# Norms with one activation table, a second attention pass over two PSUM pools, moved value matmuls, one mask product on VectorE, and another order of PSUM banks

## The chip, the cores and the metric

The kernel runs on one core of a Trainium2 chip. The metric is the device time of one execution in microseconds (us). The program computes in 32-bit floats. Its engines are named as in the profile: PE (TensorE, the matmuls), PEld (its weight loads), DVE (VectorE), ACT (ScalarE), POOL (GpSimd) and SP (SyncE, which issues most transfers). Each engine works through its own queue in order and waits on semaphores of the others. A 32-bit matmul shows in the profile as two passes, so "x16" in a row of PE is eight matmuls in the program.

## The reference, cut to what matters

Two layers over 128 latent rows of width 256, with a context of 12544 rows of width 256. Each sublayer works on a layer norm of its input and is added to it:

```python
x = x + _L0_xattn_ref(_layernorm(x), ctx, mask, Wq, Wkv, Wo)      # 4 heads of 64, masked softmax over 12544
x = x + _L0_attn_ref(_layernorm(x), ...)                          # gated delta net, 12 heads
x = x + _L0_ffn_ref(_layernorm(x), ...)                           # 8 experts, top 1
x = x + _L1_xattn_ref(_layernorm(x), ctx, Wq, bq, Wk, bk, Wv, bv) # 16 heads of 16
x = x + _L1_attn_ref(_layernorm(x), ...)                          # linear attention with decay, gate
x = x + _L1_ffn_ref(_layernorm(x), ...)                           # 8 experts, top 2

def _layernorm(x, axis=-1, eps=1e-05):
    m = jnp.mean(x, axis=axis, keepdims=True)
    v = jnp.var(x, axis=axis, keepdims=True)
    return (x - m) / jnp.sqrt(v + eps)
```

## The kernel before

The context is cut into 25 blocks of 512 rows (the last has 256), `BLOCKS`; all of them stay in SBUF. The order of the work on PE and ACT, in the first attention on DVE too, is the order in which the program writes it down (`manual_schedule`); POOL and the rest are ordered by a scheduler.

**First attention** (`xattn0_first`). PE first runs twelve spare matmuls (L371), then the keys of block 0 (`keys`, L404, into PSUM tile `pk`, copied to `kT` by ACT). The layer norm of x runs meanwhile, and calls a function handed to it (`fill`) with a number at certain places; here that function only computes the keys of block 0 when the number is 4. Then come the transposes of h (L151), the queries (`pq`, L485; scaled into `qT` by ACT, L489), scores of block 0 (`sc`, L499), of which DVE takes row maxima (L502), the values of block 0 (`values`, L417, tile `pv`), diagonals of the maxima (L510), keys of block 1, and `pn`, which spreads the maxima (L513, copied to `nm`). From there the loop takes blocks in pairs: values and keys, the weighted sum of the last pair (`weigh`, L465, tile `ot`), scores of this pair (`scores`, L438, tile `st`). A pair has four tiles of weights e: DVE subtracts the maximum (L444), ACT takes the exp (L445), POOL turns the mask's bytes into floats (`mk`, L447, two buffers) and multiplies (L451), DVE adds to the sums (L456). PSUM has three double banks for `pk`, `pv`, `st` and the like (`x0_mm`), and a pool `x0_ot` for `spare` and `ot`, opened after it.

**Fillers.** The keys and values of the second attention (`keys1`, `values1`: L1027 and L1048, copied out by ACT in L1034 and L1053) depend only on the context. `Filler.steps` yields them in small units (two passes or so of keys, two matmuls of values), and `fill(n)` puts n units on PE wherever the middle layers leave it idle. They go through two PSUM banks of their own (`k1_ps`, in place of the first attention's pools when these are closed). The middle layers are the delta net (`delta_net`, six banks) and the experts (`experts`). `layernorm` calls `fill` with 1, 4 and 1, and by `rsqrt` (L126 to L132) with 2 and 2, ten units in all; there ACT takes the logarithm and then the exponential, each after loading a table (`preload_act_table_set`) of its own.

**Second attention** (`xattn1_first`). Norm, queries, an estimate of the maxima on 128 rows (`sa`, `against`), then `fill(None)`: all units that are left, on PE one after another. Then the pools are closed and `weigh1` runs over 98 chunks of 128 context rows: `scores(i)` (L1101) writes four strips of scores, one into the tile `st1` (one buffer) and three into `st3` (two buffers), ACT takes the exps (L1107, one of 512 and one of 1536 columns), `attend(i)` (L1118) adds the weighted values into `ot`, which a zeroing matmul (L1091) has opened. The order on PE is scores 0, 1, 2, attend 0, scores 3, attend 1 and so on. One pool, `x1_st`, holds all of these tiles.

**Last layers** (`last_layers`). Here PE waits for chains of small operations; `beat(n)` puts 2n passes of a matmul on it whose result nobody reads (L1359). `root` is the norm: logarithm and exponential from one table, loaded at the end of the pass over the context (L1137), and on DVE one step of Newton's method on the inverse root (L1351, L1365).

If a check of the sums finds them out of bounds, the whole network is run once more by another path; with these inputs it is not.

Of the kernel before, what the change touches and what calls it, by code (L numbers as in the profile page):

```python
# [23 lines left out]
S = 128  # L24
# [48 lines left out]
def network(ctx: ExitStack, tc: tile.TileContext, a: dict, y_out, bad):  # L73
# [47 lines left out]

    def rsqrt(dst, src, bias, scale=1.0, fill=None):


        if fill:
            nc.scalar.preload_act_table_set("natural_log")  # L126
            fill(2)
        nc.scalar.activation(dst, src, AF.Ln, bias=bias, scale=scale)
        if fill:
            nc.scalar.preload_act_table_set("exp_and_others")  # L130
            fill(2)
        nc.scalar.activation(dst, dst, AF.Exp, scale=-0.5)  # L132

    def layernorm(x, psum, tag, fill=None):
# [5 lines left out]
        rstd = small.tile([S, 1], F32, tag="ln_rstd", name="ln_rstd")  # L140
        if fill:
            fill(1)
        rsqrt(rstd, mv[:, 1:2], eps[:S, 0:1], fill=fill)
# [205 lines left out]
    def xattn0_first(ahead, ok, filler, rest):  # L349
# [5 lines left out]
        with (  # L355
# [3 lines left out]
            tc.tile_pool(name="x0_s", bufs=1) as sp,  # L359
            tc.tile_pool(name="x0_mm", bufs=3, space=PSUM) as ps_mm,  # L360
            tc.tile_pool(name="x0_ot", bufs=1, space=PSUM) as ps_ot,
# [48 lines left out]
            def values(b):  # L410
                vs[b] = kvp.tile([128, 4, D], F32, tag="v", name="v")
                pv = two("pv")
                for i in range(BLOCKS[b][1] // 256):
                    for c in range(2):
# [12 lines left out]
            def scores(b):  # L427
# [4 lines left out]
                for c0 in range(0, n // 128, 2):  # L432
# [18 lines left out]
                    nc.gpsimd.tensor_mul(e, e, mk.unsqueeze(1).to_broadcast([128, 4, 2, S]))  # L451
# [28 lines left out]
            hT = layernorm(x, ps_one, "mm", lambda n: keys(0) if n == 4 else None)  # L480
            qT = wp.tile([128, 2, S], F32, name="qT")
            pq = two("pq")
            for m in range(2):
                for k in range(KC):
                    nc.tensor.matmul(  # L485
                        pq[:, m, :S], wq[:, k, m * 128 : (m + 1) * 128], hT[:, k, :],
                        start=(k == 0), stop=(k == KC - 1),
                    )
            nc.scalar.mul(qT, pq[:, :, :S], DH**-0.5)  # L489
# [16 lines left out]
            values(0)  # L506
# [67 lines left out]
    def delta_net(x, wqkv, fill):  # L574
# [7 lines left out]
        with (  # L582
# [136 lines left out]
            nc.scalar.preload_act_table_set("exp_and_others")  # L719
# [216 lines left out]
    def experts(x, wr, bias_row, we, be_src, top, y=None, fill=lambda n: None):  # L936

        with (
# [9 lines left out]
            hT = layernorm(x, psp, "ps", fill)  # L948
# [115 lines left out]
    def weigh1(x, qs, kss, cp, sp, loaded, late):  # L1064
# [4 lines left out]
        with (  # L1069
            tc.tile_pool(name="x1_e", bufs=1) as ep,  # L1070
            tc.tile_pool(name="x1_st", bufs=1, space=PSUM) as ps_st,
# [17 lines left out]

            ot = ps_st.tile([128, G, S], F32, name="ot")  # L1090
            nc.tensor.matmul(ot.rearrange("p g s -> p (g s)"), zl, zr, start=True, stop=False)  # L1091
# [50 lines left out]
            pt = ps_st.tile([128, 1, G, S], F32, tag="st1", name="pt")[:, 0].rearrange("p g s -> p (g s)")  # L1142
# [55 lines left out]
    def xattn1_first(x, wq, filler, close, late):  # L1198
# [3 lines left out]
        with (  # L1202
# [8 lines left out]
            with (  # L1211
# [22 lines left out]
                fill(None)  # L1234
            close()
            return weigh1(x, qs, kss, cp, sp, 2, late)
# [71 lines left out]
    def last_layers(x, w, total):  # L1308
# [4 lines left out]
        with (  # L1313
# [49 lines left out]
            beat(7)  # L1363
# [74 lines left out]
            nc.scalar.preload_act_table_set("natural_log_exp_and_others")  # L1438
# [130 lines left out]
    class Filler:  # L1569
# [3 lines left out]
        def __init__(self, kp):  # L1573
            self.kp, self.units = kp, self.steps()

# [156 lines left out]
```

## Time and profile before

| | |
|---|---|
| median of 3 runs | 768.55 us (767.87 to 768.75) |
| the profiled execution | 771.03 us |
| its span, first to last instruction | 769.0 us |
| mean granted TensorE clock | 0.994 |
| a pair of blocks in the first attention | 21.4 us |
| a chunk in the second attention | 2.1 us |

The span in stages: the first attention up to 290 us, delta net, experts and the second attention's preparation to 526, the pass over the 98 chunks to 734, the last layers to 763, and the output. The page's slices of the span, busy tenths of each engine in fortieths:

```profile
PE   8999999999999999999999999999999999999985
DVE  2444444433444444972114142000000000000045
ACT  2433433333444424654224432336999999999941
POOL 5686666667776632314012021000000000000000
```

In the queries of the timeline a row has the start, the time it takes, engine, line, operation, output and input, shapes, count, and in brackets how long the engine sat idle before it and who ended that.

### The profile page before, as it was taken

The numbers are of one execution on the slowest core, as the hardware profiler recorded it, in microseconds if no ns is written. First come the engines' busy times: TensorE is split into PE (matmuls) and PEld (weight loads), VectorE is DVE, ScalarE is ACT, GpSimd is POOL, SyncE is SP. The second block draws the span as 40 slices with busy tenths as digits, with TensorE's granted clock in tenths as the row PEclk, the third lists the DMA queues.
The fourth block names the chain that finished last, engine by engine and source line by source line (L and its number), as shares of the span: only waits on it lengthen the run. The fifth ranks groups of instructions, "written<-read, shape, count | busy, mean of one in ns | idle before, by whom it ended". The sixth has DMA issues, their size and how long they took to land.

```text
span 769.0 us, 23891 instructions
## 1 busy us (share of the span) xinstructions
PE 748.8 (97%) x10861; PEld 562.1 (73%) x10861; DVE 221.1 (29%) x405; ACT 406.9 (53%) x491; POOL 234.7 (31%) x192
## 2 busy tenths in 40 slices
PE   8999999999999999999999999999999999999985
PEld 4677777777777867666667757667888888888873
DVE  2444444433444444972114142000000000000045
ACT  2433433333444424654224432336999999999941
POOL 5686666667776632314012021000000000000000
PEclk9999999999999999999999999999999999999998
DMA  9970000000000012333010345211432222222000
GB/s 314 384 272 8 6 9 8 8 8 8 9 5 3 1 42 86 110 111 112 31 58 34 103 154 122 94 69 54 132 109 67 70 58 69 72 62 71 6 2 12
DMA packets 36126, 56.70 MB, mean 74 GB/s; under 512 B 5904, under 2 KB 12608, under 8 KB 36016
## 3 DMA queue, kind: packets, MB, share of 16 engines
q1 hardware_dynamic: 35648, 54.05, 22.0%
q8 instruction: 87, 1.43, 0.8%
q0 software_dynamic: 368, 1.03, 0.4%
q14 instruction: 23, 0.19, 0.1%
HBM read 42.09 MB, written 12.98 MB: 72 GB/s over the span
## 4 chain that ended last, share of the span: by engine, by line
PE 91%; DMA 3%; POOL 2%; ACT 2%; issue 1%; DVE 1%; SPq 0%; ACTq 0%; POOLq 0%; DVEq 0%
PE st L1101 14%; PE ot L1118 12%; PE pv L1048 11%; PE pk L1027 11%; PE pv L417 10%; PE pk L404 9%; PE st L438 6%; PE ot L465 6%; PE pr L634 1%; POOL e L451 1%; DMA msk<-in_maskT 1%; PE py L956 1%; PE spare L1359 1%; DMA row<-in_row 1%; DMA m<-in_mask 1%
## 5 line engine op out<-in xcount | busy, mean ns | idle before, releaser
L1107 ACT ACTIVATE e<-st 128x512 f32<-128x512 f32 x196 | 189.7, 1021 | 17.4 <-PE st L1101 16.1
L451 POOL TENSOR_TENSOR e<-e,mk 128x1024 f32<-128x1024 f32 x49 | 115.5, 2357 | 76.1 <-ACT e L445 62.8
L1101 PE MATMUL st<-qs,ks 32*128 32x128 f32 x3136 | 115.8, 283 | 0.8 <-ACT e L1107 0.8
L1101 PEld LDWEIGHTS st<-qs,ks 32*128 32x128 f32 x3136 | 96.9, 186 | 21.4 <-ACT e L1107 20.7
L1118 PE MATMUL ot<-e,ctx 128*17 128x128 f32 x3136 | 105.0, 274 | 0.0
L1048 PE MATMUL pv<-wv,ctx 128*128 128x256 f32 x392 | 92.8, 382 | 2.2 <-ACT kh L1034 1.6
L1027 PE MATMUL pk<-ctx,wk 128*128 128x512 f32 (+1 forms) x200 | 93.4, 591 | 0.8 <-ACT ctx L1053 0.8
L1048 PEld LDWEIGHTS pv<-wv,ctx 128*128 128x128 f32 x392 | 72.9, 190 | 23.5 <-issue 10.7
L456 DVE TENSOR_TENSOR sums<-sums,e 128x1024 f32<-128x1024 f32 x49 | 60.0, 1225 | 100.9 <-POOL e L451 100.9
L417 PE MATMUL pv<-wkv,ctx 128*128 128x256 f32 x392 | 88.3, 383 | 0.0
L1118 PEld LDWEIGHTS ot<-e,ctx 128*17 128x17 f32 x3136 | 77.6, 97 | 12.1 <-ACT e L1107 0.3
L404 PE MATMUL pk<-ctx,wkv 128*128 128x512 f32 (+1 forms) x200 | 86.4, 584 | 0.0
L445 ACT ACTIVATE e<-e 128x1024 f32<-128x1024 f32 x49 | 51.8, 1057 | 65.2 <-DVE e L444 62.4
L417 PEld LDWEIGHTS pv<-wkv,ctx 128*128 128x128 f32 x392 | 73.3, 190 | 11.7 <-PE sc L499 0.8
L447 POOL TENSOR_SCALAR mk<-msk 128x256 f32<-128x256 uint8 x49 | 68.3, 1395 | 4.1
L444 DVE TENSOR_TENSOR e<-st,nm 128x1024 f32<-128x1024 f32 x49 | 56.7, 1218 | 40.7 <-PE st L438 40.7
L1034 ACT ACTIVATE kh<-pk,col 128x512 f32<-128x512 f32 (+1 forms) x50 | 33.8, 679 | 64.7 <-PE pk L1027 63.7
L404 PEld LDWEIGHTS pk<-ctx,wkv 128*128 128x128 f32 x200 | 38.0, 190 | 40.7 <-issue 39.7
L1147 DVE RECIPROCAL den<-pt 128x16 f32<-128x16 f32 x1 | 0.3, 258 | 209.0 <-PE pt L1144 209.0
L1053 ACT COPY ctx<-pv 128x512 f32<-128x512 f32 x49 | 28.7, 586 | 53.8 <-PE pv L1048 53.7
L1027 PEld LDWEIGHTS pk<-ctx,wk 128*128 128x128 f32 x200 | 36.0, 190 | 28.4 <-issue 24.0
L408 ACT COPY kT<-pk 128x1024 f32<-128x1024 f32 (+1 forms) x25 | 24.9, 996 | 58.7 <-PE pk L404 58.7
(324 smaller groups left out, 622.9 us busy)
## 6 DMA issues: line engine op xcount, KB each, us to landing
ctx<-in_ctxT SPq DMA_DIRECT2D x24, 512.0 KB, 8.3
kd<-kh SPq DMA_DIRECT2D x48, 256.0 KB, 2.0
ks<-kd SPq DMA_DIRECT2D x192, 64.0 KB, 2.7
w<-in_L_ffn_expert_w SPq DMA_DIRECT2D x4, 512.0 KB, 3.8
ctx<-in_L_ffn_We SPq DMA_DIRECT2D x4, 512.0 KB, 4.0
msk<-in_maskT SPq DMA_DIRECT2D x24, 64.0 KB, 1.8
w<-in_L_attn_Wqk SPq DMA_DIRECT2D x2, 768.0 KB, 10.1
w<-in_L_attn_Wv SPq DMA_DIRECT2D x2, 768.0 KB, 10.1
```

What stands on the lines that cost most here:

```text
L404: nc.tensor.matmul(pk[:, m, :n], wkv[:, k, m * 128 : (m + 1) * 128], ctx_blocks[b][:, k, :], start=(k == 0), stop=(k == KC - 1),)
L417: nc.tensor.matmul(pv[:, i, c * D : (c + 1) * D], ctx_blocks[b][:, k, rows], wkv[:, k, D:], start=(k == 0), stop=(k == KC - 1),)
L444: nc.vector.tensor_add(e, st, nm.unsqueeze(2).to_broadcast([128, 4, 2, S]))
L445: nc.scalar.activation(e, e, AF.Exp)
L447: nc.gpsimd.tensor_scalar(mk, msk[:, c0 * 128 : (c0 + 2) * 128].rearrange("p (c s) -> p c s", c=2), 1.0, 0.0, ALU.mult, ALU.add,)
L451: nc.gpsimd.tensor_mul(e, e, mk.unsqueeze(1).to_broadcast([128, 4, 2, S]))
L456: nc.vector.tensor_add(sums, sums, e)
L1027: nc.tensor.matmul(pk, wk1[:, k, m * 128 : (m + 1) * 128], ctx_blocks[b][:, k, :], start=(k == 0), stop=(k == KC - 1),)
L1048: nc.tensor.matmul(pv[:, c, :], ctx_blocks[b][:, k, rows], wv1[:, k, :], start=(k == 0), stop=(k == KC - 1),)
L1101: nc.tensor.matmul(st3[:, j - 1, g, :] if j else st1[:, 0, g, :], kss[b % 3][r, g // 2, g % 2, c * 128 : (c + 1) * 128], qs[r, g, :], star ...
L1107: nc.scalar.activation(e[:, j].rearrange("p j g s -> p (j g s)"), st.rearrange("p j g s -> p (j g s)"), AF.Exp,)
L1118: nc.tensor.matmul(ot[32 * j : 32 * j + DH + 1, g, :], v[:, c, 8 * (g // 2) + 2 * j + g % 2, :], e[:, j, g, :], start=False, stop=(i + 1 = ...
```

## The change

- **One-table norms.** `layernorm` no longer goes through `rsqrt`. It loads (unless `load=False`, in the experts) one table that has logarithm and exponential, takes both on ACT right after each other, and DVE then makes one step of Newton's method on the result (four small operations, one of them before the ACT pair). Its calls of `fill` are now 3, 2, 4, 1. The same table replaces the exponential's elsewhere, so that the load at the end of the pass (L1137) is left out. The tables of silu and of the delta net's own logarithm are loaded as before.
- **First values between norm and queries.** `values` is made a generator. Half of the values of block 0 stand between the transposes and the queries, half between queries and `sc`; before, they stood after `sc`. Transposes and queries share one double bank.
- **Fourth weight's mask on VectorE.** Of the four tiles of weights of a pair, DVE multiplies the last by the mask.
- **Pass in two pools, last values in it, banks.** `x0_ot` is opened before `x0_mm`. In `weigh1` a pool with one three-bank tile `st_b` comes first, then one with `ot`, `st1` and `st_a`; the chunks use `st_a` and `st_b` in turn. The last two filler units, the values of the last block, run between scores 0 and scores 1 and use `ot`'s bank; the zeroing matmul stands after scores 2.
- **Beats.** `beat(7)` ahead of the last layers' first norm is `beat(5)`.

The diff, without empty lines and comments:

```diff
+    def log_and_exp():
+        nc.scalar.preload_act_table_set("natural_log_exp_and_others")
     def rsqrt(dst, src, bias, scale=1.0, fill=None):
...
-            nc.scalar.preload_act_table_set("exp_and_others")
+            log_and_exp()
...
-    def layernorm(x, psum, tag, fill=None):
+    def layernorm(x, psum, tag, fill=None, load=True):
...
+        ve = small.tile([S, 1], F32, tag="ln_ve", name="ln_ve")
+        nc.vector.tensor_scalar_add(ve, mv[:, 1:2], 1e-5)
+        if load:
+            log_and_exp()
         if fill:
-            fill(1)
-        rsqrt(rstd, mv[:, 1:2], eps[:S, 0:1], fill=fill)
+            fill(3)
+        nc.scalar.activation(rstd, mv[:, 1:2], AF.Ln, bias=eps[:S, 0:1])
+        nc.scalar.activation(rstd, rstd, AF.Exp, scale=-0.5)
+        t = small.tile([S, 1], F32, tag="ln_t", name="ln_t")
+        nc.vector.scalar_tensor_tensor(t, rstd, rstd, ve, ALU.mult, ALU.mult)
+        nc.vector.tensor_scalar(t, t, -0.5, 1.5, ALU.mult, ALU.add)
+        nc.vector.tensor_mul(rstd, rstd, t)
+        if fill:
+            fill(2)
...
+            tc.tile_pool(name="x0_ot", bufs=1, space=PSUM) as ps_ot,
             tc.tile_pool(name="x0_mm", bufs=3, space=PSUM) as ps_mm,
-            tc.tile_pool(name="x0_ot", bufs=1, space=PSUM) as ps_ot,
...
             def values(b):
+                for _ in value_steps(b):
+                    pass
+            def value_steps(b):
                 vs[b] = kvp.tile([128, 4, D], F32, tag="v", name="v")
                 pv = two("pv")
                 for i in range(BLOCKS[b][1] // 256):
+                    if i > 0:
+                        yield
...
-                    nc.gpsimd.tensor_mul(e, e, mk.unsqueeze(1).to_broadcast([128, 4, 2, S]))
+                    engine = nc.vector if b % 2 == 1 and c0 + 2 == n // 128 else nc.gpsimd
+                    engine.tensor_mul(e, e, mk.unsqueeze(1).to_broadcast([128, 4, 2, S]))
...
-            hT = layernorm(x, ps_one, "mm", lambda n: keys(0) if n == 4 else None)
+            first = value_steps(0)
+            shared = two("shared")
+            class Half:
+                def tile(self, shape, dtype, tag, name):
+                    return shared[:, 0, :]
+            def between(n):
+                if n == 4:
+                    keys(0)
+                elif n == 1:
+                    next(first)
+            hT = layernorm(x, Half(), "mm", between)
             qT = wp.tile([128, 2, S], F32, name="qT")
-            pq = two("pq")
+            pq = shared[:, 1, :].rearrange("p (m s) -> p m s", m=4)
...
-            nc.scalar.mul(qT, pq[:, :, :S], DH**-0.5)
+            nc.scalar.mul(qT, pq[:, :2, :], DH**-0.5)
+            for _ in first:
+                pass
...
-            values(0)
...
-            hT = layernorm(x, psp, "ps", fill)
+            hT = layernorm(x, psp, "ps", fill, load=False)
...
-    def weigh1(x, qs, kss, cp, sp, loaded, late):
+    def weigh1(x, qs, kss, cp, sp, loaded, late, rest=None):
...
+            tc.tile_pool(name="x1_sb", bufs=1, space=PSUM) as ps_sb,
             tc.tile_pool(name="x1_st", bufs=1, space=PSUM) as ps_st,
...
+            st_b = ps_sb.tile([128, 3, G, S], F32, name="st_b")
             ot = ps_st.tile([128, G, S], F32, name="ot")
-            nc.tensor.matmul(ot.rearrange("p g s -> p (g s)"), zl, zr, start=True, stop=False)
+            st1 = ps_st.tile([128, 1, G, S], F32, name="st1")
+            st_a = ps_st.tile([128, 3, G, S], F32, name="st_a")
...
-                e = ws[i % 3]
-                st1 = ps_st.tile([128, 1, G, S], F32, tag="st1", name="st1")
-                st3 = ps_st.tile([128, 3, G, S], F32, tag="st3", name="st3", bufs=2)
+                e, st3 = ws[i % 3], (st_a, st_b)[i % 2]
...
-                es = [scores(0), scores(1)]
+                es = [scores(0)]
+                if rest:
+                    rest(ot)
+                es.append(scores(1))
...
                     if i + 2 < len(chunks):
                         es.append(scores(i + 2))
+                    if i == 0:
+                        nc.tensor.matmul(ot.rearrange("p g s -> p (g s)"), zl, zr, start=True, stop=False)
                     attend(i, es.pop(0))
-                nc.scalar.preload_act_table_set("natural_log_exp_and_others")
...
-            pt = ps_st.tile([128, 1, G, S], F32, tag="st1", name="pt")[:, 0].rearrange("p g s -> p (g s)")
+            pt = st1[:, 0].rearrange("p g s -> p (g s)")
...
-                fill(None)
+                fill(filler.left - 2)
             close()
-            return weigh1(x, qs, kss, cp, sp, 2, late)
+            return weigh1(x, qs, kss, cp, sp, 2, late, filler.last)
...
-            beat(7)
+            beat(5)
...
+            self.left = sum(2 * KC + n // 128 for _, n in BLOCKS)
...
             for _ in self.units if n is None else islice(self.units, n):
-                pass
+                self.left -= 1
+        def last(self, bank):
+            self.tile = lambda shape, name: bank.rearrange("p (c g) s -> p c (g s)", c=2)
+            self.fill(None)
```

More of the change, by code (lines that the diff above doesn't have):

```diff
@@ L485, in xattn0_first @@
                     nc.tensor.matmul(
-                        pq[:, m, :S], wq[:, k, m * 128 : (m + 1) * 128], hT[:, k, :],
+                        pq[:, m, :], wq[:, k, m * 128 : (m + 1) * 128], hT[:, k, :],
                         start=(k == 0), stop=(k == KC - 1),
                     )
-            nc.scalar.mul(qT, pq[:, :, :S], DH**-0.5)
+            nc.scalar.mul(qT, pq[:, :2, :], DH**-0.5)
+            for _ in first:
+                pass
             mb0 = ep.tile([128, 1024], F32, tag="e", name="mb0")[:, :512]
@@ L718, in delta_net @@
                 nc.scalar.activation(rn, pn, AF.Ln, bias=eps[:, 1:2])
-            nc.scalar.preload_act_table_set("exp_and_others")
+            log_and_exp()
             fill(2)
@@ L1437, in last_layers @@
                 )
-            nc.scalar.preload_act_table_set("natural_log_exp_and_others")
+            log_and_exp()
             beat(2)
```

## The prediction

> **What bounds the kernel now.** I read the page's busy table first, then the list of what TensorE (PE) waited for, and then the timeline around each of those waits.
>
> ```profile
> PE 748.8 (97%) x10861; PEld 562.1 (73%) x10861; DVE 221.1 (29%) x405; ACT 406.9 (53%) x491; POOL 234.7 (31%) x192
> ```
>
> PE is busy for 97% of the span, so no work on another engine is worth anything in itself. What can be won is PE's idle time and the matmuls that compute nothing. The list of PE's waits (total, times, longest) has the candidates:
>
> ```profile
> PE pv L1048 <- ACT kh L1034: 1.6, 2, 0.9
> ...
> PE st L1101 <- ACT e L1107: 0.8, 2, 0.6
> ...
> PE ot L1091 <- issue: 0.7, 1, 0.7
> PE pv L1048 <- DVE x_xattn L570: 0.6, 1, 0.6
> PE ot L465 <- POOL e L451: 0.5, 1, 0.5
> ```
>
> The idle figures are taken against modelled ends. I size each hole by starts instead: start of the next group, less start of the group before and its passes at their undisturbed spacing. One pass is half a 32-bit matmul. Spacings from the steady loop: 32 value passes (128x256) from 45.01 to 52.02 are 0.219 us each, 16 key passes (128x512) from 52.02 to 58.98 are 0.435, 64 passes of `ot` from 58.98 to 62.62 are 0.057. In the second attention one chunk's scores take 1.10 (620.09 to 621.19) and the next step 1.00.
>
> **The change part by part.**
>
> *First values between norm and queries.* The timeline of PE at the start:
>
> ```profile
> 10.07 0.38 PE L151 MATMUL ln_pt<-ident,h 128*128 128x128 f32 x2
> 10.97 1.16 PE L485 MATMUL pq<-hT,w 128*128 128x128 f32 x8 [0.52 <-DVE hT L152]
> 12.60 1.99 PE L499 MATMUL sc<-kT,qT 64*128 64x512 f32 x8 [0.47 <-ACT qT L489]
> 22.57 0.60 PE L438 MATMUL st<-qT,kT 64*128 64x128 f32 x6
> ```
>
> PE waits for hT's copy and for qT's scaling, while the values of block 0 run later. Now eight value passes stand in each hole, 1.75 us against 0.68 and 0.78. The work from 10.07 to the first `st`: transposes 0.22, values 2 x 1.75, queries 0.91 (32 passes of `pr` from 298.99 to 302.64, eight of them), `sc` 1.92 (12.60 to 14.52), keys of block 1 3.46, `pn` and the zero matmul 1.06 (21.51 to 22.57); together 11.07, so `st` starts at 21.14: **-1.43**. The row maxima and diagonals on DVE take 3.3 us after the first `sc` is done (13.90 to 17.22). With `sc` at 14.57 they end at 19.2, and `pn` wants them at 19.95: 0.7 of cover is left; without it the rest is paid. The weights for the values were issued at 2.74, the longest landing of that tensor is 6.0 us, so they lie there at 8.74.
>
> *Fourth mask on VectorE.* Of the first pair PE waits for POOL's fourth product: `ot` x48 starts at 36.86 and its end by spacing is 39.59, the last 16 start at 40.21: **-0.62**. DVE makes the product in about 1.22 (L444 and L456, same shape, 1218 and 1225 ns); POOL needed 2.36. Its mask stands in POOL's queue one product earlier, so DVE starts at about 32.5. Behind it in DVE's queue wait the four sums, done by 38.6; nobody wants them before the next pair's e at about 42. In the steady loop DVE has nine such operations, 11 us of 21.39: no cost.
>
> *Passes over pools.* The first attention's two small banks now come first, so that the filler's two banks wait for them and not for `x_xattn`. `po` starts at 287.04, four passes end at 287.92, the next starts at 288.67: **-0.75**.
>
> *One table.* In the norms ahead of delta net and ahead of the second attention, ACT loads two tables while PE's two filler banks wait to be copied out:
>
> ```profile
> 291.32 1.28 ACT L128 ACT_TABLE_LOAD   x1
> 292.61 0.29 ACT L128 ACTIVATE ln_rstd<-ln_mv,eps 128x1 f32<-128x1 f32 x1
> 292.93 1.28 ACT L130 ACT_TABLE_LOAD   x1
> 294.22 0.59 ACT L1053 COPY ctx<-pv 128x512 f32<-128x512 f32 x1
> ```
> ```profile
> 292.20 1.88 PE L1027 MATMUL pk<-ctx,wk 128*128 128x512 f32 x4
> 294.86 1.55 PE L1027 MATMUL pk<-ctx,wk 128*128 128x512 f32 x3 [0.78 <-ACT ctx L1053]
> ```
>
> Without the loads the first hole (292.20 + 4 x 0.435 = 293.94, next start 294.86) is **-0.92** and the other (457.70 + 8 x 0.219 = 459.45, next start 460.54) **-1.09**. Added are four small DVE operations per norm, three on the norm's path: 0.22, 0.15 and 0.16 by L1351, L1365 and L1458, about 0.7 with their starts. They are covered: nine filler units, over 7 us, lie between the sum x and the transposes. Without that cover they would cost 0.7 in each of four norms. The norm ahead of the experts shows no PE wait, so it gives nothing. The holes around delta net's own tables (323.41) stay: those loads stay.
>
> *Last values in the pass, banks.*
>
> ```profile
> 523.28 1.89 PE L1048 MATMUL pv<-wv,ctx 128*128 128x256 f32 x8
> 525.89 0.37 PE L1091 MATMUL ot<-zr,zl 1*128 1x512 bf16 x1 [0.72 <-issue]
> ...
> 527.89 1.15 PE L1101 MATMUL st<-qs,ks 32*128 32x128 f32 x26 [0.61 <-ACT e L1107]
> 529.23 1.65 PE L1101 MATMUL st<-qs,ks 32*128 32x128 f32 x32 [0.19 <-ACT e L1107]
> 530.82 0.95 PE L1118 MATMUL ot<-e,ctx 128*17 128x128 f32 x27
> ```
>
> From 523.28 to the first `ot<-e,ctx` are 7.54 us. Now: scores 1.10, values 1.75, scores 1.10, then 0.2 of the third scores, a wait until the exp of the one single-buffered bank is over (0.85 after the second scores: 0.20 to its start, 0.60 long), 0.90 for the rest and about 0.3 for the zeroing matmul: 6.0. **-1.54**. The values' copy (0.59) stands in ACT's queue where ACT is idle anyway.
>
> *End of the pass.* The table load of L1137 goes: ACT's copy of `ot` started at 734.34, right behind it, and PE's last matmul ended at 734.15: **-0.15**. `beat(7)` becomes `beat(5)`, 14 passes 10:
>
> ```profile
> 736.62 4.97 PE L1359 MATMUL spare<-w,ident 128*128 128x256 f32 x14 [1.13 <-ACT total L1157]
> 741.42 0.61 PE L1371 MATMUL ln_pt<-ctx 128*128 128x128 f32 x4
> ```
> ```profile
> 736.60:740.00 3.40, 3.38 (x8) 2.76 (x9) 1.91 (x8) 0.50 (x2) 0.00 (x0) 0.50 0.01 2
> 740.00:741.40 1.40, 1.40 (x7) 1.24 (x7) 0.00 (x0) 0.00 (x0) 0.00 (x0) 0.98 0.00 0
> ```
>
> The first number after the ACT and POOL columns is PEclk: half clock until 740.0, full after. `dg`, which the next matmul needs, is done at 738.90; PE is late only by its beats. The four passes cut are the last four, at full clock: 4 x 0.219 = **-0.88**. The two-sided bound: half clock never granted, the ten passes end before `dg` and the step starts some 2.4 us earlier (-2.4); half clock twice as long, below (+0.86).
>
> **Sum.** -1.43 -0.62 -0.75 -0.92 -1.09 -1.54 -0.15 -0.88 = **-7.38**. The profiled execution took 771.03 (span 769.0 and 2.03 around it), so its like would take 763.65. The median of the runs shown, 768.55, lies 2.48 below that execution; less 7.38 it is **761.2**.
>
> **Rivals.** (a) *The clock.* The half-clock stretch of 3.4 us could last for two. Ten passes then take 10 x 0.438 = 4.38 and end at 740.85 instead of 741.21; the half clock lasts on to 743.3 and costs the 2.45 us of real matmuls half, 1.2. The tail loses 0.86 where the forecast has -1.03: -5.5, **763.1**. For it: the beats are all that PE does in that stretch, and there are fewer. Against: the beat was cold for 3.4 us and no longer. The mirror case, no cold stretch, gives -8.8: **759.7**.
>
> The Trainium skill, "TensorE: Matmul & The Clock Gate", section "What's actually happening", says that the window of about 3.4 us runs free of the kernel's start and that warm-up is a time, not a number of matmuls. The length agrees with the 3.4 us above; where the window falls no single trace can show, and by that page either case of (a) may come in some executions.
>
> (b) *ACT still blocks in order.* Ln waits for DVE's statistics, and the fillers' copies stand behind it; or the split pools wait as before. If both table holes stay, -5.4: **763.2**; if instead the pool holes stay (0.75 + 1.54), -5.1: **763.5**. Against it: the order of the instructions puts the copy of the last full bank ahead of Ln, and there the waits on `x_xattn` and on the last copy are gone.
>
> (c) *Slower.* All 196 exps of the second attention (L1107) now run under the other table. ACT has 1.94 of work in each 2.10 us chunk (two exps, 98 chunks). From 0.16 more per chunk ACT is the bound; from 0.16 + 7.38/98 = 0.235, 12% longer exps, the kernel is slower. At 20% it costs 98 x (2.33 - 2.10) = 22.5: **783.7**. Against it: the tail's exp already runs under this table (L1390, 128x128, 0.28) and takes what a copy of that size takes (L1373, 0.27).
>
> **Chances.** Forecast (760.0 to 762.4) 0.63; (a) both ways 0.13; (b) 0.17; (c) 0.04; the rest, no gain, 0.03. The likely cases all lie between 759.5 and 764.2, which is the range. Measurement tells about 0.2%, 1.5 us, from no change: faster 0.93, same 0.03, slower 0.04.
>
> **What would show it.** After: first `st` near 21.1; no PE wait on L451's successor, on `x_xattn` or on a table in the norms; steady pairs still 21.39 apart; first weighted sum of the second attention 6.0 us after the last keys; chunks still 2.10; ten beats ending 4 us after they start. I am wrong if a pair or a chunk gets longer, or if the holes reappear a few groups later with another releaser.

## The result, and the profile after

| | before | after |
|---|---|---|
| median | 768.65 us (767.87 to 771.19, 4 runs) | 762.22 us (762.06 to 762.44, 4 runs) |
| the profiled execution | 771.03 us, span 769.0 | 762.44 us, span 760.6 |
| mean granted clock of the profiled execution | 0.994 | 0.995 |

The ratio is 0.9911, with a 95% interval of 0.9888 to 0.9934: the kernel became faster by about 6.8 us, with bounds of 5.1 and 8.6 (the two medians of the table lie 6.4 apart). The prediction was 761.2 in a range of 759.5 to 764.2.

The page's busy table of the changed kernel, first line:

```profile
PE 745.8 (98%) x10857; PEld 560.8 (74%) x10857; DVE 267.0 (35%) x433; ACT 397.3 (52%) x483; POOL 179.0 (24%) x180
```

PE is busy for 3.0 us less, with the four cut passes in it, but the span is 8.4 shorter; the other 5.4 is idle time. Work has moved from POOL (234.7 before) to DVE (221.1 before): 46 us more there, of which twelve products take 40.5, a number that comes back below. The list of PE's waits in the changed kernel (total, times, longest):

```profile
PE spare L1404 <- ACT total L1202: 1.2, 1, 1.2
...
PE pv L1086 <- ACT kh L1072: 0.6, 1, 0.6
...
PE st L1141 <- ACT e L1147: 0.5, 1, 0.5
```

Gone from it are the waits on `hT`, on `qT`, on POOL's `e`, on `x_xattn` and on ACT's `ctx` ahead of the fillers' keys, and the idle time ahead of the zeroing matmul; no new releaser stands in their place. Of the two waits each on `kh` and on the exps at the start of the pass, one is left: the one at the delta net's own tables and the one on the single-buffered tile, both of which the prediction had left standing. The waits of the last layers and of the spare matmuls at the start are still there, each within 0.15 of before.

PE at the start, in the timeline of the changed kernel:

```profile
9.87 0.38 PE L167 MATMUL shared<-ident,h 128*128 128x128 f32 x2
10.09 1.89 PE L439 MATMUL pv<-wkv,ctx 128*128 128x256 f32 x8
11.82 1.05 PE L522 MATMUL shared<-hT,w 128*128 128x128 f32 x8
...
14.53 1.99 PE L538 MATMUL sc<-kT,qT 64*128 64x512 f32 x8
...
21.05 3.17 PE L460 MATMUL st<-qT,kT 64*128 64x128 f32 x52
```

No row has a bracket, so PE waits for nobody here. From the transposes to the first `st` it is 11.18 us instead of 12.50.

ACT in the norm ahead of the delta net, the rows that held two table loads before:

```profile
288.05 0.30 ACT L152 ACTIVATE ln_rstd<-ln_mv,eps 128x1 f32<-128x1 f32 x1
288.38 0.20 ACT L153 ACTIVATE ln_rstd<-ln_rstd 128x1 f32<-128x1 f32 x1
289.30 0.59 ACT L1091 COPY ctx<-pv 128x512 f32<-128x512 f32 x1 [0.71 <-PE pv L1086]
```

Logarithm and exponential now fit between two copies, and ACT waits 0.71 for the next bank instead of PE for ACT.

The first pair's weighted sum in PE's timeline, first before, then after:

```profile
36.86 2.84 PE L465 MATMUL ot<-e,v 128*64 128x128 f32 x48
40.21 1.09 PE L465 MATMUL ot<-e,v 128*64 128x128 f32 x16 [0.51 <-POOL e L451]
41.24 0.94 PE L438 MATMUL st<-qT,kT 64*128 64x128 f32 x12
```
```profile
35.34 3.71 PE L489 MATMUL ot<-e,v 128*64 128x128 f32 x64
38.98 3.84 PE L460 MATMUL st<-qT,kT 64*128 64x128 f32 x64
```

PE from `po` into the norm ahead of the delta net, after:

```profile
284.78 1.03 PE L606 MATMUL po<-wo,oT 128*128 128x256 f32 x4
285.64 3.62 PE L1086 MATMUL pv<-wv,ctx 128*128 128x256 f32 x16
289.10 3.60 PE L1065 MATMUL pk<-ctx,wk 128*128 128x512 f32 x8
292.53 1.03 PE L1086 MATMUL pv<-wv,ctx 128*128 128x256 f32 x4
```

PE at the start of the pass, with rows of the strips left out:

```profile
515.52 1.97 PE L1065 MATMUL pk<-ctx,wk 128*128 128x256 f32 x8
517.42 0.39 PE L1141 MATMUL st_a<-qs,ks 32*128 32x128 f32 x3
...
518.52 1.99 PE L1086 MATMUL ot<-wv,ctx 128*128 128x256 f32 x8
520.45 0.39 PE L1141 MATMUL st_b<-qs,ks 32*128 32x128 f32 x3
...
522.34 0.37 PE L1141 MATMUL st<-qs,ks 32*128 32x128 f32 x1 [0.50 <-ACT e L1147]
...
523.64 1.07 PE L1158 MATMUL ot<-e,ctx 128*17 128x128 f32 x32
```

The values stand between the scores. The wait of 0.50 for the exp of the single-buffered tile is the one that was foreseen. From there a chunk takes 2.10 as before.

The tail of the changed kernel, first its timeline, then its windows (busy time of PE, PEld, DVE, ACT and POOL with counts, PEclk, DMA share, GB/s):

```profile
729.05 4.11 PE L1404 MATMUL spare<-w,ident 128*128 128x256 f32 x10 [1.20 <-ACT total L1202]
732.99 0.61 PE L1416 MATMUL ln_pt<-ctx 128*128 128x128 f32 x4
```
```profile
729.00:730.00 1.00, 0.95 (x3) 0.84 (x4) 0.83 (x4) 0.03 (x1) 0.00 (x0) 0.70 0.00 0
730.00:731.00 1.00, 1.00 (x3) 0.75 (x3) 0.78 (x5) 0.47 (x2) 0.00 (x0) 0.50 0.00 0
...
732.00:733.00 1.00, 1.00 (x5) 0.79 (x4) 0.00 (x0) 0.00 (x0) 0.00 (x0) 0.59 0.00 0
```

The cold stretch, the half clock at the beats, is there again: from the shares 0.70 and 0.59 it lasts from 729.40 to 732.82, 3.4 us, and the ten beats take 3.94 to the next start.

Stage by stage, from one start to another, in the two profiled executions:

| stage | before | after | difference | predicted |
|---|---|---|---|---|
| transposes to first `st` | 12.50 | 11.18 | -1.32 | -1.43 |
| first pair, `ot` to `st` | 4.38 | 3.64 | -0.74 | -0.62 |
| `po` to the next values | 1.63 | 0.86 | -0.77 | -0.75 |
| norm ahead of the delta net, keys to values | 4.48 | 3.43 | -1.05 | -0.92 |
| norm ahead of the second attention, values to keys | 4.67 | 3.46 | -1.21 | -1.09 |
| last keys to first weighted sum | 9.34 | 8.12 | -1.22 | -1.54 |
| last weighted sums to the transposes of their result | 3.88 | 3.73 | -0.15 | -0.15 |
| those transposes to the beats | 1.85 | 1.92 | +0.07 | 0 |
| beats to `ln_pt` | 4.80 | 3.94 | -0.86 | -0.88 |
| sum | | | -7.25 | -7.38 |

That leaves about 1.15 of the 8.4 between the two spans. 0.20 fell ahead of the transposes, in the spare matmuls at the start; 0.6 in the delta net and experts between the two norms, of which PE's "issue" gaps in the 32x32 matmuls (L853), in which it waits for nothing that the profile shows, explain 0.5 (2.4 in total before, 1.9 after, and anywhere from 1.2 to 2.4 in the kernels below, which run the same matmuls there); 0.3 between the first weighted sum and the last three, where chunks lie 2.10 or 2.11 apart in both kernels but for one of 2.42 and one of 2.21 before and one of 2.21 after. The remaining differences are under 0.1. None of this is a wait on another engine that came or went with the change; why one chunk took 2.42 stays open.

### The profile page after: what moved, and what is told of

It reads as the page before. It is cut to its first block, busy times and chain, and to the rows that moved or that the text cites. A ratio compares the mean times of both kernels' runs of the same rounds, so it can differ in the third digit from the quotient of the medians.

```text
span 760.6 us, 23856 instructions
## 1 busy us (share of the span) xinstructions
PE 745.8 (98%) x10857; PEld 560.8 (74%) x10857; DVE 267.0 (35%) x433; ACT 397.3 (52%) x483; POOL 179.0 (24%) x180
## 3 DMA queue, kind: packets, MB, share of 16 engines
q8 instruction: 87, 1.43, 0.8%
## 4 chain that ended last, share of the span: by engine, by line
PE 97%; ACT 1%; DVE 1%; issue 0%; POOL 0%; ACTq 0%; DVEq 0%; POOLq 0%
PE ot L1158 13%; PE pv L439 11%; PE pk L1065 11%; PE pv L1086 11%; PE pk L420 11%; PE st_b L1141 7%; PE st_a L1141 7%; PE st L460 6%; PE ot L489 6%; PE pr L672 1%; PE py L994 1%; PE st L1141 1%; PE spare L1404 1%; PE pg L802 1%; PE py L1518 1%; PE pout L968 1%
## 5 line engine op out<-in xcount | busy, mean ns | idle before, releaser
L475 POOL TENSOR_TENSOR e<-e,mk 128x1024 f32<-128x1024 f32 x37 | 87.5, 2366 | 130.5 <-issue 116.7
L1141 PE MATMUL st<-qs,ks 32*128 32x128 f32 x784 | 113.0, 283 | 0.5 <-ACT e L1147 0.5
L1141 PEld LDWEIGHTS st<-qs,ks 32*128 32x128 f32 x784 | 94.4, 186 | 0.7 <-ACT e L1147 0.7
L1086 PE MATMUL pv<-wv,ctx 128*128 128x256 f32 x384 | 90.6, 382 | 0.6 <-ACT kh L1072 0.6
L439 PE MATMUL pv<-wkv,ctx 128*128 128x256 f32 x392 | 88.4, 382 | 0.0
L439 PEld LDWEIGHTS pv<-wkv,ctx 128*128 128x128 f32 x392 | 73.2, 190 | 10.9
L466 DVE TENSOR_TENSOR e<-st,nm 128x1024 f32<-128x1024 f32 x49 | 56.6, 1218 | 49.8 <-PE st L460 49.8
L1147 ACT ACTIVATE e<-st_a 128x1536 f32<-128x1536 f32 x49 | 70.8, 1445 | 0.0
L1147 ACT ACTIVATE e<-st_b 128x1536 f32<-128x1536 f32 x49 | 70.8, 1444 | 0.0
L1147 ACT ACTIVATE e<-st 128x512 f32<-128x512 f32 x98 | 58.7, 598 | 17.0 <-PE st L1141 17.0
L480 DVE TENSOR_TENSOR sums<-sums,e 128x1024 f32<-128x1024 f32 x49 | 63.1, 1288 | 5.7 <-POOL e L475 3.6
L1141 PE MATMUL st_a<-qs,ks 32*128 32x128 f32 x1176 | 57.3, 283 | 0.0
L1141 PE MATMUL st_b<-qs,ks 32*128 32x128 f32 x1176 | 57.2, 283 | 0.0
```

Source lines behind the costliest of these rows:

```text
L439: nc.tensor.matmul(pv[:, i, c * D : (c + 1) * D], ctx_blocks[b][:, k, rows], wkv[:, k, D:], start=(k == 0), stop=(k == KC - 1),)
L466: nc.vector.tensor_add(e, st, nm.unsqueeze(2).to_broadcast([128, 4, 2, S]))
L475: engine.tensor_mul(e, e, mk.unsqueeze(1).to_broadcast([128, 4, 2, S]))
L480: nc.vector.tensor_add(sums, sums, e)
L1086: nc.tensor.matmul(pv[:, c, :], ctx_blocks[b][:, k, rows], wv1[:, k, :], start=(k == 0), stop=(k == KC - 1),)
L1141: nc.tensor.matmul(st3[:, j - 1, g, :] if j else st1[:, 0, g, :], kss[b % 3][r, g // 2, g % 2, c * 128 : (c + 1) * 128], qs[r, g, :], star ...
```

## The experiments

The question was whether the sum is made of the parts named, or whether other effects happen to add up to it. So each part was undone alone. Each kernel below is the changed kernel with one part edited. The ratios stand against the kernel before, run in the same lot (runs taken together on one chip); beside the median stands the distance from start to start in the kernel's own profile.

### The same kernel again

> The changed kernel once more, not an instruction different. It shows how much one kernel's profile moves by itself. Theory (the clock's windows fall differently in each execution): first keys start somewhere between 6.0 and 7.1 us, the ten beats ahead of the last norm take either 2.43 (full clock) or about 4 (half clock), and all the other distances stay as they were: 11.18 from the transposes to the first st, 3.64 and 3.43 and 3.46 at the mask and the norms, 2.10 a chunk, each within 0.1. Median 762.2, ratio 0.991. Rival (the clock belongs to the kernel): the beats take 3.9 to 4.1 again and the first keys start at 6.44.

Measured: 761.39 us (760.52 to 763.50, 6 runs), ratio 0.9901 (0.9883 to 0.9920). In its profile (PE's timeline at the start and in the tail):

```profile
7.08 3.96 PE L420 MATMUL pk<-ctx,wkv 128*128 128x512 f32 x8
...
729.78 2.42 PE L1404 MATMUL spare<-w,ident 128*128 128x256 f32 x10 [1.20 <-ACT total L1202]
```

The theory holds. With not an instruction changed, the first keys start at 7.08 (6.44 in the first profile) and take 0.36 longer (3.79 to the transposes at 10.87 against 3.43), and the ten beats take 2.34 to the start of `ln_pt` (732.12), without a cold stretch. The table's other distances repeat: 11.18, 3.64, 0.86, 3.43, 3.45 and 8.12. So one kernel's executions differ by up to 3 us, as much as the largest two terms of the sum together, while a distance inside a profile repeats within 0.03 here as long as no change of the clock falls into it. For parts of about 1 us the verdict has to come from the distances. The expectations for the parts below were written before this was known and go by medians.

### First values back behind `sc`

```diff
-                elif n == 1:
-                    next(first)
...
-            for _ in first:
-                pass
...
+            for _ in first:
+                pass
```

> The changed kernel with the values of block 0 behind the first scores again. Theory: the two holes of PE around the queries come back, 1.3 to 1.45 us longer. Rival (what PE gains there it waits for later, on the maxima, the masks or the transfers of the first pairs): under 0.3 us longer.

Measured: 761.97 us (761.21 to 763.94, 4 runs), 0.9914 (0.9888 to 0.9940). By the median the part would be worth nothing. PE's timeline:

```profile
10.47 1.16 PE L520 MATMUL shared<-hT,w 128*128 128x128 f32 x8 [0.52 <-DVE hT L168]
12.10 1.99 PE L533 MATMUL sc<-kT,qT 64*128 64x512 f32 x8 [0.47 <-ACT qT L524]
```

Both holes are back with the lengths of before, and the distance is 12.50 again (9.57 to 22.07): the part is worth 1.32. The four runs spread over 2.7 us, so their median can't show a part of this size; in the profiled one (761.21) the transposes came early, at 9.57, and the beats ran at full clock, which more than makes up for the loss.

### All mask products on POOL

```diff
-                    engine = nc.vector if b % 2 == 1 and c0 + 2 == n // 128 else nc.gpsimd
+                    engine = nc.gpsimd
```

> The changed kernel with all mask products on POOL. Theory: POOL's fourth product of the first pair is late again by 0.6 us, once; 0.6 us longer. Rival (the product on VectorE costs something in every pair): the same or shorter, with pairs shorter than 21.39 us.

Measured: 762.81 us (761.53 to 763.15, 4 runs), 0.9911 (0.9888 to 0.9935). The first weighted sum in PE's timeline:

```profile
39.23 1.09 PE L489 MATMUL ot<-e,v 128*64 128x128 f32 x16 [0.50 <-POOL e L475]
```

From `ot` at 35.88 to `st` at 40.25 it takes 4.37 instead of 3.64: the part is worth 0.73, and the wait on POOL is its cause. Later pairs stay 21.39 apart (65.41 to 86.80) as in the changed kernel (64.14 to 85.53), so the product on VectorE costs nothing in the pairs.

### Pools of the first attention in the old order

```diff
-            tc.tile_pool(name="x0_ot", bufs=1, space=PSUM) as ps_ot,
             tc.tile_pool(name="x0_mm", bufs=3, space=PSUM) as ps_mm,
+            tc.tile_pool(name="x0_ot", bufs=1, space=PSUM) as ps_ot,
```

> The changed kernel with the first attention's two PSUM pools in the old order. Theory: the fillers behind it wait for the sum x again, 0.75 us longer. Rival (the wait turns up at the next bank anyway): no difference.

Measured: 762.27 us (761.26 to 762.96, 4 runs), 0.9911 (0.9887 to 0.9935). PE's timeline:

```profile
285.92 3.69 PE L1086 MATMUL pv<-wv,ctx 128*128 128x256 f32 x16 [0.60 <-DVE x_xattn L608]
```

`po` starts at 284.29: 1.63 instead of 0.86, worth 0.77. Nothing but the order in which two pools are opened decides whose banks the fillers get, and so whom they wait for.

### Two tables in the norms

```diff
-        if load:
-            log_and_exp()
...
-        nc.scalar.activation(rstd, mv[:, 1:2], AF.Ln, bias=eps[:S, 0:1])
-        nc.scalar.activation(rstd, rstd, AF.Exp, scale=-0.5)
-        t = small.tile([S, 1], F32, tag="ln_t", name="ln_t")
...
+        rsqrt(rstd, mv[:, 1:2], eps[:S, 0:1], fill=fill)
...
+                nc.scalar.preload_act_table_set("natural_log_exp_and_others")
```

The exponentials' table and the numbers handed to `fill` are the old ones again too.

> The changed kernel with the norms' two tables again (no step of Newton's method, the load at the end of the pass too). Theory: the two holes of PE behind ACT's table loads come back, 0.92 + 1.09, and 0.15 at the end of the pass: 2.2 us longer. Rival (Ln in ACT's queue holds the filler copies just as long without loads): under 0.5 us longer.

Measured: 765.24 us (763.53 to 766.41, 6 runs), 0.9948 (0.9932 to 0.9964). It is the only part whose median stands apart, though its interval still touches that of the changed kernel's first runs (up to 0.9934). ACT in the norm ahead of the delta net:

```profile
290.29 1.28 ACT L134 ACT_TABLE_LOAD   x1
291.58 0.59 ACT L1079 COPY ctx<-pv 128x512 f32<-128x512 f32 x1
```

This is the second of two loads, the first starting at 288.68; the copy PE waits for stands behind both. The distances are 4.44 at this norm (289.60 to 294.04, +1.01) and 4.66 at the other (454.22 to 458.88, +1.20); with the end of the pass (3.87 from the last weighted sums to the transposes of their result, +0.14) this is 2.35, where 2.2 was expected. The wait at the delta net's own tables grows as well, from 0.62 to 1.18. That 0.56 is not a part of what the change won, since the kernel before waits 0.62 there with the same tables; why it grows was not traced. The median lies 3.0 above the changed kernel's first one, which is of another lot.

### Last values and zeroing ahead of the pass

```diff
-            tc.tile_pool(name="x1_sb", bufs=1, space=PSUM) as ps_sb,
...
-            st_b = ps_sb.tile([128, 3, G, S], F32, name="st_b")
...
+            nc.tensor.matmul(ot.rearrange("p g s -> p (g s)"), zl, zr, start=True, stop=False)
...
+            st_b = ps_st.tile([128, 3, G, S], F32, name="st_b")
...
-                if rest:
-                    rest(ot)
...
-                    if i == 0:
-                        nc.tensor.matmul(ot.rearrange("p g s -> p (g s)"), zl, zr, start=True, stop=False)
...
-                fill(filler.left - 2)
+                fill(None)
```

> The changed kernel with the pass over the context in one pool again: the last values ahead of it, the zeroing matmul first. Theory: the wait on the values' copy and the two on the single-buffered bank come back; 1.5 us longer. From the last keys to the first weighted sum 7.5 us where the changed kernel has 6.3. Rival (the start of the pass is bound by ACT's exps anyway, so the holes move behind it): under 0.5 us longer, with waits of the same length in the first ten chunks of the changed kernel.

Measured: 763.00 us (761.69 to 763.58, 4 runs), 0.9911 (0.9893 to 0.9929). PE's timeline:

```profile
520.84 0.37 PE L1130 MATMUL ot<-zr,zl 1*128 1x512 bf16 x1 [0.72 <-issue]
...
522.84 0.37 PE L1141 MATMUL st<-qs,ks 32*128 32x128 f32 x1 [0.61 <-ACT e L1147]
```

The first weighted sum starts at 525.76. The distance is that of before to 0.01 (7.53 from the values at 518.23, 9.34 from the keys at 516.42). The part is worth 1.22 and not 1.54.

### How many beats

Three kernels with `beat(7)`, `beat(3)` and `beat(0)` in place of `beat(5)`:

```diff
-            beat(5)
+            beat(7)
```

> The changed kernel with seven beats again. Theory (the half clock lasts for about 3.4 us from the first beats, whatever PE does in them): the four passes put back run at full clock, 4 x 0.219 = 0.88 us; the beats take 4.8 instead of 3.94 us, the time is 0.9 us longer than the changed kernel's. Rival (cutting beats gained nothing, because the matmuls behind them stayed cold for as long): no difference.

Measured: 762.91 us (761.73 to 763.55, 4 runs), 0.9912 (0.9894 to 0.9930). Its profile had no cold stretch at the beats, so 14 passes took 3.12 to the next start, less than ten cold ones. Against the 2.34 of ten passes at full clock, in the repeat above, the four passes cost 0.78; the 4.8 expected for a cold stretch was not put to the test.

```diff
-            beat(5)
+            beat(3)
```

> The changed kernel with three beats, six passes. The diagonal that the next matmul needs is done 2.27 us after the first beat. Theory (a fixed stretch of half clock): the beats end at about 2.3 to 2.6 us, the next matmul starts there and not at 3.94, the matmuls run cold until 3.4 us after the first beat at double time (some 0.5 us more); 0.6 to 1.0 us shorter than the changed kernel. Rival (PE warms up by the work it is given): the half clock lasts a second stretch of 3.4 us, the same or up to 1 us longer.

Measured: 761.62 us (761.50 to 762.11, 4 runs), 0.9898 (0.9881 to 0.9914). The six passes ran at full clock, PE then waited 0.77 for the diagonal, and the next matmul starts 2.33 after the first beat, as with ten passes at full clock (2.34). The median is 1.3 below that of `beat(7)` in the same lot, but the intervals overlap; with no cold stretch in the profile neither theory nor rival was put to the test.

```diff
-            beat(5)
+            beat(0)
```

> The changed kernel without beats ahead of the last layers' first norm: PE idles until the diagonal is done. Theory (a fixed stretch that ends by itself): like three beats, 0.6 to 1.0 us shorter than the changed kernel. Rival (the stretch only ends after 3.4 us in which PE works): half clock for 3.4 us of real matmuls, which then take some 1.5 us more; 0 to 1 us longer than the changed kernel.

Measured: 763.55 us (763.24 to 764.05, 4 runs), 0.9922 (0.9905 to 0.9938). Here the rival won: all four runs are slower than all of `beat(3)`'s, and their mean clocks, 0.992 and 0.993, are lower than in any other run of this lot (0.995 at the least). The interval still overlaps with that of `beat(7)`. Windows of this kernel, columns as above, with 0.50 in all those between:

```profile
730.00:731.00 1.00, 0.00 (x0) 0.00 (x0) 0.71 (x5) 0.50 (x2) 0.00 (x0) 0.72 0.00 0
...
737.00:738.00 1.00, 1.00 (x9) 1.00 (x9) 0.36 (x1) 0.60 (x2) 0.00 (x0) 0.87 0.00 0
```

From the shares 0.72 and 0.87 the half clock ran from 730.44 to 737.26, 6.8 us, twice the length seen above. PE idled for 3.63 until the first real matmul, and the real matmuls fell into the cold: the keys of the last attention took 1.84 to the next start instead of 0.99. The beats are not idle decoration; without them the next work pays.

### Matmuls in the holes ahead of the beats

If idle time makes the clock fall, the two holes behind the pass (0.48 and 1.20) may be where the tail's cold stretch comes from. PE has nothing to do there but wait for ACT.

```diff
+                nc.tensor.matmul(gap, ident, kss[0][:, 0, 0, :256], start=True, stop=True)
                 for g in range(G):
                     nc.tensor.transpose(pt[:, g * 128 : (g + 1) * 128], oT[:, g, :], ident)
+                for _ in range(2):
+                    nc.tensor.matmul(gap, ident, kss[0][:, 0, 0, :256], start=True, stop=True)
```

`gap` is a bank of the tile `st_a`, which nobody reads any more. The order of these lines is kept by `manual_schedule`.

> One unused matmul (two passes) in the hole before the transposes of the second attention's result and two (four passes) in the hole behind them, so that PE idles about 0.3 us there instead of 1.68; beat(5) stays. They cost nothing, since PE waits there for copies on ACT. Theory (the half clock follows from the idle time in the 3.4 us before it): the ten beats run at full clock, 2.43, no half clock anywhere behind the pass; the median falls by the mean of what the cold executions lose, 0 to 0.9 us, to 761.4 to 762.2. Rival (the half clock falls wherever its window falls): in part of the executions the beats are still cold, and the median stays at 762.2.

Measured: 761.36 us (760.42 to 761.75, 5 runs), 0.9896 (0.9878 to 0.9914). PE's timeline:

```profile
727.49 0.71 PE L1192 MATMUL st<-ident,oTs 128*128 128x128 f32 x4
728.04 1.03 PE L1194 MATMUL st_a<-ks,ident 128*128 128x256 f32 x4
729.40 2.43 PE L1409 MATMUL spare<-w,ident 128*128 128x256 f32 x10 [0.33 <-ACT total L1207]
```

The ten beats ran at full clock, as the theory said; but so they did in most profiles without these matmuls.

> The same with beat(3) in place of beat(5): six passes, about 1.3 us at full clock, then PE waits about 0.8 for the diagonal. Theory: about as fast as with five beats at full clock less 0.9, so 761.0 to 761.6; both the tail's distance from the last matmul of the pass to ln_pt, 6.27 in the changed kernel's profile, comes to 5.3. Rival (fewer beats let the clock fall): half clock in the keys behind the norm, 1 us more than with five beats.

Measured: 760.86 us (759.96 to 761.99, 5 runs), 0.9894 (0.9875 to 0.9913). The beats start at 728.83 and `ln_pt` at 731.17: 2.34, as with ten passes at full clock (729.40 to 731.74 above) and in the repeat of the unedited kernel. The diagonal sets this distance, PE waits 0.78 for it, and no half clock falls on the matmuls behind it. Counted from the end of the weighted sums, where the first of the unused matmuls starts (726.37), the tail of the kernel with three beats takes 4.80; in the changed kernel's first profile, with the same 3.18 from the start of the last three weighted sums, it took 6.41. That profile had the cold stretch: in the repeat without one the distance is 4.80 too (727.32 to 732.12), and with ten beats behind the filled holes it is 4.80 (726.94 to 731.74). So the unused matmuls and the fewer beats shorten nothing where the clock is full; all that they could win is the cold stretch.

Of all that was run this has the lowest median, but its interval and those of the kernel itself overlap, so that it is faster is not shown. The medians do not decide for the theory either (761.36 against 761.39). The mean granted clock says a little more, since a cold stretch of 3.4 us lowers it by 0.002: of the 36 runs of kernels with the two holes and at least five beats, fourteen were below 0.997 (eleven of them at 0.995); of the ten runs with the holes filled, none was. That speaks for the theory; it is not proof, because the share of 0.995 differed much between kernels (3 of 4 in the changed kernel's first runs, none of 4 in the one with the values ahead of the pass), and because the mean also takes in the output at the end, where PE has nothing to do and the clock falls too (0.50 from 757.0 in the changed kernel's profile).

### Why the mask product is so slow on VectorE

In the changed kernel the twelve products on DVE take 3.37 us each, not the 1.22 reckoned. Two rows that start together, one of DVE's timeline and one of POOL's:

```profile
48.36 3.37 DVE L475 TENSOR_TENSOR e<-e,mk 128x1024 f32<-128x1024 f32 x1 [3.55 <-POOL mk L469]
```
```profile
48.29 2.36 POOL L475 TENSOR_TENSOR e<-e,mk 128x1024 f32<-128x1024 f32 x1
```

POOL ends at 50.65, DVE 1.08 later. In the kernel before, the timelines of DVE and POOL have it the other way round:

```profile
47.25 1.23 DVE L456 TENSOR_TENSOR sums<-sums,e 128x1024 f32<-128x1024 f32 x1 [0.19 <-POOL e L451]
```
```profile
47.31 1.44 POOL L447 TENSOR_SCALAR mk<-msk 128x256 f32<-128x256 uint8 x1
```

The conversion that takes 0.41 by itself takes 1.44 beside DVE's sum and ends 0.27 after it. To see whether the product is slow or is held up, all products went to DVE:

```diff
-                    engine = nc.vector if b % 2 == 1 and c0 + 2 == n // 128 else nc.gpsimd
+                    engine = nc.vector
```

> All 49 mask products on VectorE, none on GpSimd, which only turns the mask's bytes into floats. It asks why the twelve products on VectorE take 3.37 us each in the changed kernel, where 1.22 was reckoned; each of them runs beside a product on GpSimd that ends 1.08 us before it does (51.73 against 50.65). Theory (the two engines do not read SBUF at the same time, and VectorE's product waits until GpSimd's is through): with no product on GpSimd each takes about 1.22, or up to 1.7 where a conversion of 0.41 falls into it; DVE has about 12 x 1.25, 15 us, of work in a pair of 21.39, the pairs stay, and the time is that of the changed kernel, 761 to 763. Rival (the product itself is slow on VectorE, its second operand being one row of mask repeated four times): 3.37 each, alone too; four of them with the subtractions and sums make 4 x (1.22 + 3.37 + 1.33) = 23.7 per pair, DVE becomes the bound, and each of the twelve pairs grows by 2.3: about 790.

Measured: 795.79 us in a single run, 769.56 for the kernel before beside it. DVE's groups by line (mean ns of one behind the total):

```profile
L475 DVE TENSOR_TENSOR e<-e,mk 128x1024 f32<-128x1024 f32 x49 | 60.0, 1224 | 59.3 <-ACT e L467 59.3
```

Without a product on POOL each takes 1.224: it is held up, not slow. So the theory is right about the cause. Its time is wrong by 33 us, and the rival's 790 is near for a wrong reason: neither side had counted the order in DVE's queue. A product waits 1.19 for its exp, and in DVE's queue the next tile's subtraction stands behind it; tiles now follow each other every 3.55 us, PE waits 26.8 us for them (L439 on DVE's L466, 14 times), and a pair takes 23.84 (50.07 to 73.91).

## Why the prediction was right

**The sum.** The mechanisms were those named, each with its undo: removing a part brings back the wait with the releaser of before and its length to 0.04 (two tables in the norms bring back 0.56 more at the delta net); the beats are a term without a wait. The eight terms came to -7.32 in the profiles, with the 0.07 that one row lost to -7.25, against -7.38. One piece of this is luck: both profiled executions met a cold stretch at the beats. Had the first profile of the changed kernel been like its repeat, that row would be -2.46 (4.80 to 2.34), near the bound of -2.4 that the prediction gave for it, and the sum -8.85. The other rows do not hang on the clock.

**First values, mask, pools, norms.** Off by 0.11, 0.12, 0.02, 0.13 and 0.12. The hole ahead of `sc`, put at 0.78, is 0.72 by the step's own numbers (12.60 less 10.97 and 0.91); the sum did not use it. The covers named held. The diagonals ended at 19.15 (19.2 was said) and `pn` started at 19.99. The Newton operations ended at 289.22 and h at 289.70, 3.7 before the transposes at 293.39. The copy of the full bank stood ahead of the logarithm, so rival (b) did not come.

**Start of the pass, -1.54: the term that was mis-sized.** It is -1.22, in the comparison and in the undo alike. The step counted the values as 8 x 0.219 = 1.75 between two sets of scores. They take 1.93 (518.52 to 520.45), and the keys before the scores 1.90 (515.52 to 517.42) where the same eight passes ahead of the values took 1.80. Going from a 128x256 matmul to strips of 32 rows costs 0.10 to 0.18 in these rows; 0.28 of the missing 0.32 is there, and the new order does it twice where the old one did it once, inside a wait.

**Mask on VectorE, "about 1.22".** The term was right, its cost was not: 3.37. It stayed hidden because DVE had the room that the step named; the four sums ended at 39.08 (38.6 was said) and the next pair's e was wanted at 40.19.

**Rival (c), exps slower under the other table.** The exps' groups have means of 598 and 1444 ns before, 598 and 1444 to 1445 after, and chunks stay 2.10 apart (523.64, 525.74). It is refuted.

**Rival (a), the clock.** The mirror case is real: in the profiles of most kernels run here the beats met no half clock; in the changed kernel's first they did, in its repeat not. It is not a rival result of the change but a part of every measurement. The Trainium skill's "TensorE: Matmul & The Clock Gate", section "What's actually happening", has the window run free of the kernel's start; the executions of one and the same kernel with and without the cold stretch agree with that. The case "twice as long" came only with `beat(0)`.

**Against the median.** The forecast took the sum from the median of before. The first lot gave 762.22, 1.0 above it, and three of its four runs had the clock of 0.995; the repeat gave 761.39. Both are the same kernel, so 0.8 of the missing 1.0 lies within what one kernel's lots differ by, and no term of the sum is off by as much.

## What to carry to other kernels

When PE is busy for 97% of the span, work through the holes one by one from start to start, and undo each by itself; a distance inside the profile, with no change of the clock in it, repeats within a few hundredths where the total swings by 3 us. Before moving work from one engine to another, look for pairs of rows on the two engines that overlap in time and last longer than alone, and count what stands behind the moved instruction in its new queue. Filler that keeps the clock up is worth its time only until the next step's own input is there: six passes were enough here, fourteen made that step late, and with none the real matmuls ran cold.

## What the runs showed of the hardware

VectorE and GpSimd hold each other up: a DVE product with both inputs in SBUF took 3.37 us beside a product on POOL and 1.224 without, and POOL's conversion 1.44 beside a DVE sum and 0.41 without. The later of the two waits for nearly the whole of the other: it ends 1.08 and 0.27 after the other's end, 0.14 less than it takes without it. The Trainium skill, "SBUF — State Buffer", section "Who interferes with whom", says that a VectorE instruction with two inputs in SBUF and a GpSimd instruction that reads SBUF exclude each other for a whole instruction, and that the one that starts first goes through; both pairs of rows agree, with POOL 0.07 ahead in the one and DVE 0.06 in the other.

The granted clock falls to half for 3.4 us at the beats (736.6 to 740.0 before, 729.40 to 732.82 after) and for 6.8 us in the kernel without beats (730.44 to 737.26). The twelve spare matmuls at the start, the same in every kernel, took between 4.0 and 5.3 us, and the first keys started anywhere from 5.88 to 7.08.
